# Two AdaLN blocks on one core: the setup ahead of the attention moved into the hand-written order of slots

## The chip, the core and the metric

The kernel runs on one core of a Trainium2 chip. The time is device microseconds of one launch. Five runs of the kernel before gave a median of 1122.37 us (1118.46 to 1125.07). The engines are PE (TensorE), DVE (VectorE), ACT (ScalarE), POOL (GpSimd) and SP (SyncE), which only issues DMAs here.

## What is computed

Two transformer blocks on `x` of 8 batches, 512 tokens and 128 channels, all in 32-bit floats. Only the start of the first block matters for the change:

```python
mod = (_silu(L0_c) @ L0_wmod).reshape(L0_c.shape[0], 6, 1, -1)
sa, ca, ga, sb, cb, gb = (mod[:, i] for i in range(6))
ga = (2 * (ga >= 0) - 1) * jnp.maximum(jnp.abs(ga), 0.25)   # gb likewise
h = _layernorm(x, axis=-1) * (1 + ca) + sa
x = x + ga * attention(h)        # 16 heads of 8 channels, weights W + 2 B A (low rank)
h = _layernorm(x, axis=-1) * (1 + cb) + sb
x = x + gb * mixture_of_experts(h)
```

The second block has the same frame with a state-space layer and another mixture of experts, and its own `mod`.

## The kernel before, in words

**Setup (lines 97 to 350).** Batches lie as tiles `x0` to `x7`, 128 tokens on partitions, four chunks. SP loads the columns `pc` (L103) and all eight batches (L107). ACT issues `wqkvo`, `lora` and `wmod` (L114 to L118), POOL twelve later weights (L120 to L143). DVE makes the constants (`tri`, `ones`, `before`, `count`, `mask`, `spare`), POOL clears `zeros`, four `mpad` tiles of 128x512 (L185) and two `vaug` tiles of 128x2048. PE makes the modulation of both layers (L210, two times six matmuls of 128x128 by 8 columns), the low-rank product (L232), the output bias (L237), and the gate rows (L249): four tensors of a row per batch, each as two groups of four 128x128 matmuls that spread a column over all partitions; ACT copies each group to `ga_rows`, `gab_rows`, `sb_rows`, `cb_rows` (L252). DVE takes the statistics of all eight batches (L261, L262). `finish_stats` then makes all 32 reciprocal roots at once: ACT Sqrt (L265) and DVE reciprocal (L266).

In this part a scheduler chooses the order of the instructions on each engine: its order is not that of the program. The statistics of eight batches stand mixed with the modulation on DVE, and Sqrt behind the first five gate-row copies on ACT.

**Attention (from L350).** From here the order is written out by hand: the wrapper `InOrder` (its line, L65, stands for all instructions issued through it) pins each engine to program order, and PE's matmuls are pinned one by one. Work is told off in slots. `slot(s)` issues two score matmuls `ps` (from slot 0 on, L474) and one pair `pm` (L446), whose row maxima DVE takes (`mpad<-pm`), twelve slots ahead of the scores (`LEAD` is 6 steps of two slots); then the Exp of the scores on ACT (`es<-ps`), and what `at_slot` has put behind this slot. `pm` has two buffers, the one-bank PSUM tiles (`bank`) four. A `pm` or `ps` matmul has 32 rows of the array, and two or four of them stream side by side; transposes, projections and gate rows use all 128 rows.

For batch 0, `load_batch` normalises the four chunks on POOL (`xh`, slot -30), PE transposes them (`ptn`), ACT modulates (`ht`), PE projects (`pqk`, L406), ACT evicts `qf` and `kf`, and `split` masks four heads of a group (`qt`, `kt`) on POOL. The first slot with PE work is -12. `max_done` transposes the maxima of a group (`pmt`, L462, slot -3 for the first) and DVE subtracts them from `qt`. Every 32 slots are a batch. In slots 0, 2, ... SP also issues sixteen fills of 1 MB that zero `x_rows`, which the mixture of experts scatters into from slot 84 on.

## Time and profile before

| | us |
|---|---|
| median of five runs | 1122.37 |
| the profiled execution, its own time | 1121.07 |
| its span, first to last instruction | 1119.3 |
| PE busy | 1023.3 (91%) |
| DVE busy | 665.0 (59%) |
| ACT busy | 633.4 (57%) |
| POOL busy | 471.1 (42%) |
| DMA, mean over the span | 81 GB/s |
| mean granted clock of TensorE | 0.945 |

A busy share is a mean over stages of different kinds; a busy PE is not PE at its peak, since matmuls are pipelined and their ends are modelled. The granted clock is the share of full speed that PE was given. In the timeline a row has its start, its length, engine, line, operation, output and input, the number of instructions merged into it, and in brackets the idle time of that engine ahead of it and what ended it. A matmul in 32-bit floats has two records, a transpose one.

### The profile page before, as it was taken

The numbers are of one execution on the slowest core, as the hardware profiler recorded it, in microseconds if no ns is written. First come the engines' busy times: TensorE is split into PE (matmuls) and PEld (weight loads), VectorE is DVE, ScalarE is ACT, GpSimd is POOL, SyncE is SP. The second block draws the span as 40 slices with busy tenths as digits, with TensorE's granted clock in tenths as the row PEclk, the third lists the DMA queues.
The fourth block names the chain that finished last, engine by engine and source line by source line (L and its number), as shares of the span: only waits on it lengthen the run. The fifth ranks groups of instructions, "written<-read, shape, count | busy, mean of one in ns | idle before, by whom it ended". The sixth has DMA issues, their size and how long they took to land. (4 is left out here: it accounts for less than half of the span.)

```text
span 1119.3 us, 24186 instructions
## 1 busy us (share of the span) xinstructions
PE 1023.3 (91%) x9540; PEld 667.8 (60%) x9540; DVE 665.0 (59%) x1356; ACT 633.4 (57%) x1378; POOL 471.1 (42%) x723
## 2 busy tenths in 40 slices
PE   6799999999999999999989999959989956878887
PEld 6255555555555555555579999747778724444555
DVE  4377776776777777777420023026676469697563
ACT  2156666676766667666735565324576544555543
POOL 4401223462544546352463033436432374456570
PEclk9589999999999999999989999959999977989999
DMA  9960000000000000000047677511553032232241
GB/s 305 283 175 2 2 1 12 1 28 4 16 16 9 23 5 28 1 28 4 16 151 203 179 200 203 145 38 43 146 145 101 8 107 77 76 95 96 81 145 38
DMA packets 92033, 90.60 MB, mean 81 GB/s; under 512 B 6769, under 2 KB 71353, under 8 KB 91921
## 3 DMA queue, kind: packets, MB, share of 16 engines
q1 hardware_dynamic: 86928, 78.31, 23.7%
q0 software_dynamic: 4688, 9.68, 2.8%
q8 instruction: 75, 1.23, 0.5%
q10 hardware_dynamic: 304, 1.08, 0.3%
q14 instruction: 38, 0.30, 0.1%
HBM read 57.71 MB, written 31.33 MB: 80 GB/s over the span
## 5 line engine op out<-in xcount | busy, mean ns | idle before, releaser
L65 DVE TENSOR_REDUCE mpad<-pm 128x2 f32<-128x1024 f32 x256 | 309.8, 1221 | 136.5 <-PE pm L446 122.7
L65 ACT ACTIVATE es<-ps 128x512 f32<-128x512 f32 x512 | 275.1, 598 | 157.1 <-PE pm L446 111.6
L474 PE MATMUL ps<-qt,kt 32*128 32x512 f32 x1024 | 292.5, 635 | 0.1
L446 PE MATMUL pm<-kt,qt 32*128 32x512 f32 x1024 | 280.6, 664 | 4.5 <-POOL kt L65 2.4
L495 PEld LDWEIGHTS av<-es,vaug 128*32 128x32 f32 x4096 | 104.3, 109 | 94.4 <-ACT part L65 41.0
L495 PE MATMUL av<-es,vaug 128*32 128x128 f32 x4096 | 138.2, 276 | 0.0
L474 PEld LDWEIGHTS ps<-qt,kt 32*128 32x128 f32 x1024 | 95.3, 185 | 61.1 <-issue 33.3
L65 ACT ACTIVATE hid<-ph,bias 128x256 f32<-128x256 f32 x184 | 72.2, 477 | 56.7 <-PE ph L947 55.0
L708 POOL DMA_INDIRECT x_rows<-tok,ux x64 | 64.4, 1007 | 75.9 <-DMA x_rows<-tok,ux 69.6
L958 PEld LDWEIGHTS pyb<-w2b,hid 128*128 128x128 f32 x736 | 91.1, 194 | 6.0 <-ACT hid L65 3.3
L958 PE MATMUL pyb<-w2b,hid 128*128 128x128 f32 x736 | 91.8, 278 | 2.9 <-ACT hid L65 2.9
L446 PEld LDWEIGHTS pm<-kt,qt 32*128 32x128 f32 x1024 | 79.6, 190 | 24.6 <-DVE mpad L65 11.2
L947 PE MATMUL ph<-xt,w1b 128*128 128x256 f32 x368 | 89.6, 387 | 1.9 <-issue 1.9
L65 POOL TENSOR_SCALAR qt<-qf,mask,zero 128x512 f32<-128x512 f32 x32 | 24.6, 769 | 149.8 <-PE pm L446 128.4
L978 POOL DMA_INDIRECT yg<-y_rows,yrows x64 | 63.1, 987 | 35.6 <-issue 17.9
L65 DVE COPY xt<-pxt 128x256 f32<-128x256 f32 x46 | 19.4, 421 | 98.3 <-PE pxt L873 80.0
L947 PEld LDWEIGHTS ph<-xt,w1b 128*128 128x128 f32 x368 | 68.0, 195 | 9.8 <-issue 2.1
L1374 PE MATMUL pe<-x,l1w_sb 128*128 128x512 f32 x128 | 71.4, 666 | 0.5 <-ACT ye L65 0.3
L65 ACT ACTIVATE ye<-pe,pc 128x512 f32<-128x512 f32 x64 | 43.4, 683 | 40.5 <-PE pe L1374 31.7
L65 POOL TENSOR_TENSOR t<-t 128x512 f32<-128x512 f32 x34 | 49.3, 1450 | 36.3 <-DVE t L65 21.3
L65 DVE TENSOR_TENSOR t<-ye,gb 128x512 f32<-128x512 f32 x64 | 53.2, 848 | 4.6 <-POOL t L65 4.6
L1362 PE MATMUL r<-l1w_sb,t 128*128 128x128 f32 x240 | 33.9, 287 | 14.7 <-POOL t L65 9.4
(318 smaller groups left out, 1537.2 us busy)
## 6 DMA issues: line engine op xcount, KB each, us to landing
x_rows<-zeros SPq DMA_DIRECT2D x16, 1024.0 KB
gb<-g_rows SPq DMA_DIRECT2D x32, 512.0 KB
w1b<-in_w1t SPq DMA_DIRECT2D x46, 256.0 KB
w2b<-in_w2t SPq DMA_DIRECT2D x46, 256.0 KB
xg<-x_rows SPq DMA_DIRECT2D x46, 128.0 KB
y_rows<-yb SPq DMA_DIRECT2D x46, 128.0 KB
x<-in_x SPq DMA_DIRECT2D x8, 256.0 KB
h_chan<-hf SPq DMA_DIRECT2D x8, 256.0 KB
```

The costliest lines, as they stand in the source:

```text
L65: return lambda *args, **kwargs: self.pin(call(*args, **kwargs))
L446: T.matmul(pm[:, i, :], lhsT=qt[r : r + 32, qc * P : (qc + 1) * P], rhs=kt[r : r + 32, :], start=True, stop=True,)
L474: T.matmul(ps, lhsT=kt[r : r + 32, kc * P : (kc + 1) * P], rhs=qt[r : r + 32, :], start=True, stop=True)
L495: T.matmul(ps[32 * j : 32 * j + 32, 0, :], lhsT=vaugs[b % 2][:, kc, 4 * j + m, :], rhs=es_of[4 * g + kc, j][:, q], start=(kc == 0), stop=( ...
L708: nc.gpsimd.indirect_dma_start(out=x_rows[h], out_offset=IndirectOffsetOnAxis(ap=chosen["ux", b][:, k, c : c + 1], axis=0), in_=half[h]["t ...
L947: pin(T.matmul(ph[:, f, :], lhsT=it["w1"][:, f * P : (f + 1) * P], rhs=it["x"], start=True, stop=True))
L958: T.matmul(py[:, c, :], lhsT=it["hid"][:, f, c * P : (c + 1) * P], rhs=it["w2"][:, f, :], start=(f == 0 and "shared" not in it), stop=(f = ...
L978: nc.gpsimd.indirect_dma_start(out=gathered[b][:, k, c, :], out_offset=None, in_=y_rows[h], in_offset=IndirectOffsetOnAxis(ap=half[h]["yro ...
L1362: T.matmul(ffn[b]["r"][:, c, :], lhsT=x[:, c * P : (c + 1) * P], rhs=w, start=(start and c == 0), stop=stop, skip_group_check=True,)
L1374: pin(T.matmul(pe, lhsT=l1w_sb[:, 2 + e, :], rhs=x1s[b], start=True, stop=True))
```

## The change

- The whole setup is pinned to program order on DVE, ACT, POOL and SP; PE's setup matmuls are pinned too.
- SP loads `pc`, `x0`, then `wmod` of layer 0 in two pieces, `x1`, `wmod` of layer 1, the other batches and after them the twelve later weights, which POOL issued before. ACT issues `wqkvo` and `lora` (two pieces). The early weights no longer have a pool of their own; they use buffers of `es`.
- `zeros`, `mpad` and `vaug` are cleared on DVE instead of POOL.
- Statistics are taken one batch per 32 slots (`load_stats`, slots 32b-40 to 32b-37), and the roots per batch (`load_root`, slot 32b-35) by a power on POOL and a Newton step, on DVE for batch 0 and on POOL for the others. Sqrt, its table and the reciprocal go.
- Silu comes at slot -42, the low-rank product at -34, layer 0's modulation at -33. Its gate clamp (-11), the output bias (-10), layer 1's modulation (-9) and clamp (-8) come behind the first `pm`. The eight gate-row groups are one per slot from -8 to -1.
- Batch 0's `xh` and the first group's `qt` and `kt` are made on DVE instead of POOL; batch 0 gets `gab_rows` at slot -2 instead of -27.

On PE the order is now: low-rank product, modulation 0, `ptn`, `pqk`, three slots of `pm`, bias, a slot of `pm`, modulation 1, and then `pm`, gate-row group, in turn, eight times; `pmt` stands between the `pm` and the gate rows of slot -3.

```diff
-    V, A, G, T, Q = nc.vector, nc.scalar, nc.gpsimd, nc.tensor, nc.sync
+    pin = tc.keep_in_program_order
+    V, A, G, Q = (InOrder(e, pin) for e in (nc.vector, nc.scalar, nc.gpsimd, nc.sync))
+    T = nc.tensor
...
-    G.memset(zeros, 0.0)
+    V.memset(zeros, 0.0)
...
-        G.memset(mp, 0.0)
+        V.memset(mp, 0.0)
...
-    def finish_stats(mv, rstd):
-        A.activation(rstd, mv[:, :, 1], AF.Sqrt, bias=eps5)
-        V.reciprocal(rstd, rstd)
...
-    for b in range(B):
-        stats(xs[b], mv1, b)
-    finish_stats(mv1, rs1)
...
-            G.memset(va, 0.0)
-            G.memset(va[:, :, :, HD], 1.0)
+            V.memset(va, 0.0)
+            V.memset(va[:, :, :, HD], 1.0)
...
+        wmod_sb = []
+        for layer in range(2):
+            parts = []
+            for c0 in range(0, 6 * D, S):
+                w = min(S, 6 * D - c0)
+                t = early([P, w], f"wmod{layer}")
+                Q.dma_start(out=t, in_=wmod[:, layer, c0 : c0 + w])
+                parts += [t[:, k * D : (k + 1) * D] for k in range(w // D)]
+            wmod_sb.append(parts)
+            load_x(layer + 1)
+        for b in range(3, B):
+            load_x(b)
+        load_later()
...
+        def mod_rows(src, dst, b0):
+
+            pg = bank("prow")
+            for b in range(b0, b0 + 4):
+                pin(
+                    T.matmul(
+                        pg[:, b - b0, :], lhsT=src[:, b : b + 1].to_broadcast([P, P]), rhs=ident, start=True, stop=True
+                    )
+                )
+            A.copy(dst[:, b0 : b0 + 4, :], pg)
...
+        def load_root(b):
+            r = rs1[:, b * NC4 : (b + 1) * NC4]
+            on = V if b == 0 else G
+            root_end(r, root_begin(r, mv1[:, b * NC4 : (b + 1) * NC4, 1], 1e-5, on=on), on=on)
...
-                    G.tensor_scalar(
+                    (V if b == 0 else G).tensor_scalar(
...
+            on = V if g == 0 else G
+            on.tensor_scalar(qt, batch[b]["q"], mask[:, m : m + 1], zero, ALU.mult, ALU.add)
+            on.tensor_scalar(kt, batch[b]["k"], mask[:, m : m + 1], spare[:, sp : sp + 1], ALU.mult, ALU.add)
...
+        at_slot(-42, silu_c)
+        at_slot(-34, low_rank)
+        at_slot(-33, lambda: modulation(0, mod0))
+        at_slot(-11, lambda: clamp(mod0, MOE_SCALE))
+        at_slot(-10, out_bias)
+        at_slot(-9, lambda: modulation(1, mod1))
+        at_slot(-8, lambda: clamp(mod1, None))
+        rows = ((gab, gab_rows), (mod0[:, 2, :], ga_rows), (mod0[:, 3, :], sb_rows), (mod0[:, 4, :], cb_rows))
+        for i, (src, dst) in enumerate(rows):
+            for b0 in range(0, B, 4):
+                at_slot(-8 + i + b0, lambda src=src, dst=dst, b0=b0: mod_rows(src, dst, b0))
...
+            for c in range(NC4):
+                at_slot(32 * b - 40 + c, lambda b=b, c=c: load_stats(b, c))
+            at_slot(32 * b - 35, lambda b=b: load_root(b))
+            for i, s in enumerate((-30, -27 if b else -2, -24)):
```

## The prediction, on record before the run

> **What bounds the kernel now.** I read first the 40 slices of the page, to see where engines, clock and transfers change, then the timeline of the first 75 us, where the change lies, and last a table of busy time by stretches cut to the steps of the granted clock.

> ```profile
> PE   6799999999999999999989999959989956878887
> PEclk9589999999999999999989999959999977989999
> DMA  9960000000000000000047677511553032232241
> ```

> The reader is to see that PE is full from slice 3 to half of the span, while the first two slices (28 us each) are setup: PE waits there, and in slice 2 its clock stands at half. What the setup loses is lost to the end, since the attention behind it keeps PE full. The DMA row is near 9 in the same slices, mostly the zero fill of `x_rows` (16 x 1 MB), which nobody needs until the first scatter (slot 84).

> In the timeline I follow the last waits up to the first matmul of the pipeline (`pm`, slot -12):

> ```profile
> 25.68 0.58 ACT L252 COPY sb_rows<-p 128x512 f32<-128x512 f32 x1 [0.31 <-PE p L249]
> 26.29 1.28 ACT L265 ACT_TABLE_LOAD   x1
> 27.58 0.32 ACT L265 ACTIVATE rstd_l0a<-mv_l0a,eps 128x32 f32<-128x32 f32 x1
> ...
> 27.93 0.35 DVE L266 RECIPROCAL rstd_l0a<-rstd_l0a 128x32 f32<-128x32 f32 x1 [4.59 <-ACT rstd_l0a L265]
> ...
> 28.40 3.15 POOL L65 TENSOR_SCALAR xh<-x,mv_l0a,rstd_l0a 128x128 f32<-128x128 f32 x4 [6.54 <-DVE next L65]
> ...
> 32.16 0.78 ACT L65 ACTIVATE ht<-ptn,mod 128x512 f32<-128x512 f32 x1 [2.81 <-issue]
> ...
> 36.81 0.69 ACT L65 ACTIVATE qf<-pqk,bqs 128x512 f32<-128x512 f32 x1 [3.87 <-PE pqk L406]
> 37.40 0.68 ACT L65 ACTIVATE kf<-pqk,pc 128x512 f32<-128x512 f32 x1
> ...
> 38.35 0.79 POOL L65 TENSOR_SCALAR kt<-kf,mask,spare 128x512 f32<-128x512 f32 x1
> ...
> 39.19 2.09 PE L446 MATMUL pm<-kt,qt 32*128 32x512 f32 x8 [2.42 <-POOL kt L65]
> ```

> One batch's roots wait for the statistics of all eight, and the square root waits on ACT behind five gate-row copies and a table load. Only at 28.40 does batch 0 start, and at 39.19 the first `pm`. Slot 0 (first `ps`, after a `qt` update) streams at 59.43: 20.2 us for twelve slots, 1.7 each.

> **The clock in this stage.** The records of the clock begin at 23.94 (the 1.00 that the views show earlier is a default: 16 gate-row records of L249 took 3.76 us at 18.20 and 32 took 3.74 us at 24.59). It changes only at multiples of 3.41 us from there. Columns: PE, PEld, DVE, ACT, POOL busy, then granted clock.

> ```profile
> 34.18:37.59 3.41, 2.60 (x4) 0.50 (x2) 0.00 (x0) 0.78 (x2) 0.00 (x0) 0.50 0.97 283
> 47.83:51.24 3.41, 3.21 (x12) 1.01 (x8) 2.36 (x2) 0.00 (x0) 0.00 (x0) 0.50 0.97 282
> 58.07:61.48 3.41, 3.41 (x14) 1.18 (x8) 2.32 (x3) 0.10 (x1) 0.00 (x0) 0.50 0.98 283
> 61.48:64.90 3.42, 3.42 (x18) 2.07 (x16) 1.80 (x3) 1.59 (x4) 0.00 (x0) 0.50 0.97 280
> 64.90:68.31 3.41, 3.41 (x30) 1.87 (x24) 2.41 (x3) 2.68 (x6) 0.00 (x0) 1.00 0.97 283
> ```

> Busy time does not decide: 3.21 of 3.41 us busy leaves the clock at half. What sorts the steps is how much of the array streams. A record of 512 columns streams 0.853 us at half clock, one of 128 columns 0.213, weighted by its rows over 128. A window of `pm` alone (32 rows) uses 0.50 of the array, 34.18 and 58.07 use 0.70, and all stay at half; 61.48, with `ps` and `pm` side by side, uses 0.99 and is followed by full clock. Over the whole trace every half-clock window up to 0.70 stayed and every one from 0.83 up was released (0.83 at 948.95, a quarter of the array's time in it being transposes, so these count); full-clock windows below 0.31 fell back and from 0.44 up stayed.

> **The setup, new path.** In program order DVE sets the pace. It does the small constants of before (0.81 to 1.2 us), waits for `ident` (2.53 in before, behind one DMA issue that goes: about 1.6), then the scan, mask and counts, as 15.40 to 16.3 and 1.18 to 1.6 of before: to 3.0. New on DVE are POOL's memsets. DVE's own rows give 0.11 us for 64 and 0.17 for 128 elements, about 1 ns an element: four `mpad` of 512, 2.1, and two `vaug` of 2048 with their ones, 4.4: 9.6 with `next`. POOL's rows (0.54 and 1.80) would give 9.0; two elements a step, as DVE's 0.45 us for a 32x512 TENSOR_SCALAR suggests, 6.4. I take 9.6, from the nearest rows. Statistics of batch 0 alone: 4 x 0.26, 10.7. `x0` landed at 5.06 in before, so its transfer is covered by 4 us. The root: DVE 0.2, POOL power 1.05 to 1.44 (`rstd_l0f`, `rr`), four DVE steps of 0.2: 13.0. Then `wqk` 0.6, `bqs`, `mod` copy and two adds 0.3, and `xh` on DVE, four of 0.2 to 0.28: 14.8, against 3.15 us on POOL. The modulation matmuls (12 records of 0.22 us after a weight that should land by 6) are done by 9. From the last `xh` to `ht` before took 0.62 us, from `ht` to `kf`'s end 5.92, all the same; `kt` on DVE 0.46 to 0.8 in place of 0.79 after a `qt`. First `pm` at 21.9 in place of 39.19: **-17.3 us**, between -14.5 (POOL-like small steps) and -20 (fast memsets). Neither table load nor Sqrt is on this path; the Exp table load (1.28) moves behind the last gate-row copy, where `ps` of slot 0 streams beside it.

> **What the slots take over.** PE is in order, so work put into slots -10 to -1 stands between `pm` and `pm`. Eight gate-row groups of 8 records: 1.71 us each at half clock. A change between 32-row and 128-row work also drains:

> ```profile
> 56.02 1.12 PE L462 MATMUL pmt<-ident,mpad 128*128 128x128 f32 x4
> 57.07 2.57 PE L446 MATMUL pm<-kt,qt 32*128 32x512 f32 x8
> ```

> By the records, `pm` stopped streaming at 55.88, `pmt` streamed from 56.08 to 56.93, `pm` from 57.23: gaps of 0.2 and 0.3. A slot with a row group thus takes 1.71 + 0.2 + 1.71 + 0.3 = 3.9 us at half clock against 1.7: 2.2 x 8 = 17.7. The second modulation (12 x 0.213 and a drain, 3.1), the bias matmul (0.8) and the first slots' lost overlap (1.8) make 23.4. DVE's additions there (17 small operations at 0.08, four statistics at 0.27) fit under PE's 3.9 a slot. ACT's eight copies of 0.59 too. Bounds: nothing, if the rows ran in holes (PE has 0.2 us idle in 3.41, so no), to 23.4.

> [...]

> How much of the 23.4 comes back hangs on the clock. A row slot uses (1.71 + 0.85) / 3.9 = 0.65 of the array, a best-placed window 0.71: just above what stayed. At slot -3 the transposes `pmt` (0.85) stand beside a row group (1.71): such a window reaches 0.83 if it lies right, 0.75 in nearly half of the placements. If released there, the last two row slots cost 4.2 in place of 8.0, and the first scores, at half clock for 5.5 us in before, save 2.7: 23.4 - 6.5 = **+16.9**.

> **The rest.** Seven batches' statistics (4 x 0.27 each) go onto DVE inside the attention, and seven roots of some 2.3 us onto POOL, which there waits 87 us for `pm`. DVE is busy 36 of 50 us, PE paces: of at most 7.4 us I take **+1.2**; a gain I exclude, as nothing leaves. The 12 later weights (SP, about 0.4 us an issue) now stand ahead of the zero fill, same bytes, needed 100 us later: 0. `gab` is added to `x0` late (slot -2), on POOL, before splits that have 5 us to spare: 0.

> **Sum.** -17.3 + 16.9 + 1.2 = +0.8 on the profiled execution's 1121.07 us (span 1119.3). The median of before is 1.30 above it, so 1122.37 + 0.8 = **1123.2**.

> **The rivals.**
> *Cold to slot 0 (slower).* No window reaches the bound, because transposes and rows straddle two. Then 23.4 stand, less 0.8 for a release soon after slot 0: -17.3 + 22.6 + 1.2 = +6.5, 1128.9. It decides as soon as the clock is still at half when the first `ps` streams. For it: 0.65 is below 0.70.
> *Early release (faster).* The bound lies near 0.70 and the second row slot ends it: six row slots at 2.0 instead of 3.9 save 11.4, `pmt` 0.4, the first scores 2.7: -17.3 + 8.9 + 1.2 = -7.2, 1115.2. For it: 0.71 is in reach of the bound.
> *Setup does not shorten.* A transfer on the shared queue (x0, or weights for `mod`) lands later than DVE needs it; it must be 5 us late to matter, and each us costs one. At 5 us more: 1128.

> [...]

> **How the numbers follow.** Late release 0.42 (its own range 1119 to 1127, by the setup's bounds); cold 0.33; early release 0.19; setup not shorter 0.06. A difference of 0.3% (3.4 us) is what a measurement can tell here. Faster by that: early release and 0.08 of the late one, 0.27. Slower: 0.31 of cold, 0.07 of late, 0.03 of the last, 0.41. Same: 0.32. The range, from the early release with a larger setup gain to cold with a smaller one: 1113 to 1131.

> **What would show it.** First `pm` at 21 to 23 us; `vaug` memsets of about 2 us on DVE; row slots of 3.9 us while the clock is at half; a release next to `pmt` of slot -3; first `ps` near 61 (65 if cold, 53 if early). I am wrong if the clock is full in the first row slots, if gate rows stream beside `pm`, or if the attention's batches (62.1 us from `es` to `es` of 32 slots now) lengthen by over 1 us each.

## The result, and the profile after

The changed kernel took 1124.5 us (median of 36 runs, 1120.47 to 1130.21) beside 1120.86 us for the kernel before in the same series (62 runs, 1117.19 to 1125.08): a ratio of 1.0032 with a 95% interval of 1.0023 to 1.0041, slower by 0.3% or 3.6 us. The profiled execution took 1125.72 us, its span is 1123.9.

The 40 slices of the changed kernel:

```profile
PE   4999999999999999999979999859989966968887
PEclk9999999999999999999989999969899977889999
DMA  9970000000000000000047677511543032222241
```

In slice 2 PE is full, where it waited before. The clock row is no help there: the records of this execution begin at 59.43, and ahead of them the views show full clock whatever it was. The lengths tell it: eight records of 128 columns take 1.16 us at full clock, 2.08 at half.

The timeline of the same kernel, up to the first `pm` (start, length, engine, line, operation, output and input, idle time ahead):

```profile
5.46 2.00 DVE L65 MEMSET vaug<- 128x2048 f32 x2 [0.38 <-issue]
...
9.77 0.29 DVE L65 BATCH_NORM_STATS2 bnst<-x 128x6 f32<-128x128 f32 x1
10.19 0.26 DVE L65 BATCH_NORM_STATS2 bnst<-x 128x6 f32<-128x128 f32 x1
...
11.74 1.02 POOL L65 TENSOR_TENSOR rstd_l0a<-var,mhalf 128x4 f32<-128x4 f32 x1 [10.32 <-DVE var L65]
...
23.02 1.23 PE L469 MATMUL pm<-kt,qt 32*128 32x512 f32 x4 [2.20 <-DVE kt L65]
```

DVE paces this stretch without a pause over 0.4 us up to the statistics, and POOL idles for 10.3 us until DVE has a variance. `pm` starts at 23.0, 16.2 us ahead of before. The row slots of the same kernel, on PE:

```profile
51.67 2.08 PE L385 MATMUL prow<-ident,gab 128*128 128x128 f32 x8
53.68 2.08 PE L469 MATMUL pm<-kt,qt 32*128 32x512 f32 x4
55.69 1.12 PE L485 MATMUL pmt<-ident,mpad 128*128 128x128 f32 x4
56.59 1.91 PE L385 MATMUL prow<-ident,mod 128*128 128x128 f32 x8
58.44 1.60 PE L469 MATMUL pm<-kt,qt 32*128 32x512 f32 x4
59.97 1.16 PE L385 MATMUL prow<-ident,mod 128*128 128x128 f32 x8
...
63.20 0.70 PE L497 MATMUL ps<-qt,kt 32*128 32x512 f32 x2
```

From 35.62 on `pm` and gate rows alternate every 4.0 us at half clock; the clock is full from 59.43, the end of the window (one of the 3.41 us steps of the clock) that holds most of `pmt`, and the last row slot takes 2.14. The first `ps` streams at 63.20, before at 59.43: the 16.2 us won ahead of the first `pm` are lost, and 3.8 more, in the twelve slots behind it.

Where the rest goes is read from the distance of like instructions in the two traces (ACT's, counted back from the last). It needed more than one profile of each kernel; the others are among the experiments. All distances are to the first profile of before, in us:

| | at 100 us | at 560 | at 600 | at the end |
|---|---|---|---|---|
| before, second profile | +0.1 | 0.0 | +0.5 | +3.0 |
| before, third profile | +1.3 | +1.0 | +1.4 | +4.4 |
| changed kernel | +2.0 | +1.7 | +3.5 | +4.6 |
| changed kernel, again | +0.7 | +0.6 | +2.4 | -0.7 |

Three things are to be seen. From 60 to 100 the changed kernel makes up 1.8 us of what it lacked at the first `ps`, since its clock is full by then and that of before isn't until 64.9. Between 100 and 560 nothing is lost to the statistics in the attention. Between 560 and 600, where the attention ends, the changed kernel loses 1.8 us, in both of its profiles; before loses at most 0.4. What comes behind 600 spreads by 4 us between executions of one kernel and says nothing on the change.

### The profile page after: what moved, and what is told of

It reads as the page before. It is cut to its first block, busy times and chain, and to the rows that moved or that the text cites. A ratio compares the mean times of both kernels' runs of the same rounds, so it can differ in the third digit from the quotient of the medians.

```text
span 1123.9 us, 24218 instructions
## 1 busy us (share of the span) xinstructions
PE 1030.0 (92%) x9540; PEld 671.2 (60%) x9540; DVE 677.7 (60%) x1373; ACT 632.5 (56%) x1376; POOL 470.3 (42%) x739
## 5 line engine op out<-in xcount | busy, mean ns | idle before, releaser
L65 DVE TENSOR_REDUCE mpad<-pm 128x2 f32<-128x1024 f32 x256 | 310.6, 1219 | 128.6 <-PE pm L469 128.1
L65 ACT ACTIVATE es<-ps 128x512 f32<-128x512 f32 x512 | 275.0, 598 | 134.9 <-PE pm L469 112.8
L65 ACT ACTIVATE hid<-ph,bias 128x256 f32<-128x256 f32 x184 | 72.2, 477 | 58.0 <-PE ph L985 55.6
L65 DVE COPY xt<-pxt 128x256 f32<-128x256 f32 x46 | 19.3, 421 | 98.1 <-PE pxt L911 84.8
L65 POOL TENSOR_SCALAR qt<-qf,mask,zero 128x512 f32<-128x512 f32 x31 | 24.1, 776 | 125.9 <-PE pm L469 100.3
L985 PEld LDWEIGHTS ph<-xt,w1b 128*128 128x128 f32 x368 | 67.9, 195 | 10.3 <-issue 2.2
L65 ACT ACTIVATE ye<-pe,pc 128x512 f32<-128x512 f32 x64 | 43.4, 683 | 40.7 <-PE pe L1412 31.9
L65 POOL TENSOR_TENSOR t<-t 128x512 f32<-128x512 f32 x34 | 49.5, 1457 | 36.3 <-DVE t L65 21.3
L65 DVE TENSOR_TENSOR t<-ye,gb 128x512 f32<-128x512 f32 x64 | 53.2, 848 | 4.6 <-POOL t L65 4.6
L996 PE MATMUL pyb<-ws,hid 128*128 128x128 f32 x256 | 39.1, 299 | 15.2 <-issue 14.9
```

Source lines behind the costliest of these rows:

```text
L65: return lambda *args, **kwargs: self.pin(call(*args, **kwargs))
L985: pin(T.matmul(ph[:, f, :], lhsT=it["w1"][:, f * P : (f + 1) * P], rhs=it["x"], start=True, stop=True))
L996: T.matmul(py[:, c, :], lhsT=it["hid"][:, f, c * P : (c + 1) * P], rhs=it["w2"][:, f, :], start=(f == 0 and "shared" not in it), stop=(f = ...
```

## Experiments

The theory: two costs meet. DVE's chain sets the first `pm`; behind it the gate rows are serial with `pm` on PE, and a row slot costs 4.0 us rather than 2.1 because a mix of `pm` and rows uses too little of the array to bring the clock back (0.65 to 0.67 in the four windows of the changed kernel from 35.53 to 49.19, an estimate made as in the prediction). The main rival: the clock is no part of it, rows cost what they cost. The runs fell on four chips (before takes 1092 to 1093 us on two of them, 1121 to 1124 on the others), so times are compared as ratios to before on the same chip; a distance to the changed kernel is that ratio over 1.0032.

| kernel | first `pm` | first `ps` | ratio to before, 95% interval |
|---|---|---|---|
| changed kernel again | 22.9 | 61.9 | 1.0030, 1.0010 to 1.0049 |
| rows in one block, early | 30.1 | 50.3 | 0.9925, 0.9901 to 0.9948 |
| clears on POOL | 18.6 | 57.7 | 1.0019, 0.9997 to 1.0040 |
| no rows | 23.0 | 48.3 | 0.9911, 0.9887 to 0.9934 |
| fillers | 21.1 | 61.5 | 0.9941, 0.9908 to 0.9974 |
| more fillers | 21.1 | 49.4 | 0.9900, 0.9883 to 0.9917 |
| rows early, clears on POOL | 27.4 | 47.4 | 0.9894, 0.9880 to 0.9909 |
| the same, with fillers | 26.7 | 49.6 | 0.9893, 0.9879 to 0.9908 |
| the same, clamp late | 26.9 | 44.9 | 0.9867, 0.9842 to 0.9892 |
| later weights on POOL | 23.0 | 66.5 | 1.0029, 1.0011 to 1.0048 |

**Rows in one block ahead of the first `pm`.**

```diff
-                at_slot(-8 + i + b0, lambda src=src, dst=dst, b0=b0: mod_rows(src, dst, b0))
+                at_slot(-15, lambda src=src, dst=dst, b0=b0: mod_rows(src, dst, b0))
```

(The first clamp and the bias move ahead with it, to slot -23, and the second modulation to -14.)

> All eight groups of gate-row matmuls are put in one block after the first projections and ahead of the first power product pm, instead of one group beside each of eight slots. Theory (the eight row groups are serial on PE and slow only because the clock is at half while pm and rows alternate at 0.50 to 0.67 of the array): the rows run dense, 8 x 1.7 = 13.7 us at half clock or less, the first pm moves from 23.0 to 29 to 31, the twelve slots ahead of the first ps then cost 1.2 to 1.7 us each without rows, and the first ps starts at 46 to 51 instead of 63.2; the time is 8 to 15 us under the changed kernel's. Rival (the rows cost the same wherever they stand, and the clock is no part of it): first ps within 2 us of 63.2, time within 0.3% of the changed kernel's.

The gate rows on PE, in this kernel's timeline:

```profile
20.62 2.97 PE L385 MATMUL prow<-ident,gab 128*128 128x128 f32 x16
23.43 5.52 PE L385 MATMUL prow<-ident,mod 128*128 128x128 f32 x48
```

The 64 records take 8.3 us in all: they follow the projections without a gap, and the clock is full from 22.74, where the first dense window ends. `pm` starts 7.1 us later, `ps` 12.9 us earlier, the time is 1.1% or 12 us under the changed kernel's, as expected. The rival is out: where the rows stand decides their price. (The clamp, the bias and the second modulation moved with them and have a part in the figure.)

**No rows.** The gate-row matmuls and copies are left out, and the rows are filled with 0.5, so the gates are not computed.

```diff
-                at_slot(-8 + i + b0, lambda src=src, dst=dst, b0=b0: mod_rows(src, dst, b0))
+                at_slot(-8 + i + b0, lambda dst=dst, b0=b0: G.memset(dst[:, b0 : b0 + 4, :], 0.5))
```

> The gate-row matmuls and their copies are left out, and the rows are filled with 0.5 by GpSimd: the gates are not computed. Theory (the row groups cost what stands on PE ahead of the first ps): first ps at 45 to 48 instead of 63.2, some 15 us less, and the time 13 to 17 us under the changed kernel's, with the attention's batches as long as before. Rival (the start is set by the statistics and by the chain from pm to es, with the rows in its shadow): first ps not more than 5 us earlier.

The first `ps` at 48.34 is 14.9 us ahead of the changed kernel, the time 13.6 us under it. Against it the dense block costs 2.0 us at the first `ps` (the bias and the second modulation, which moved along, take less there and lower the figure); spread over the slots the same rows cost 14.9.

**Fillers.** Two kernels put matmuls of no use on PE ahead of the rows.

```diff
+        def fill_pe(n):
+            for _ in range(n):
+                pin(T.matmul(flat(bank("fill")), lhsT=ident, rhs=xs[0].rearrange("p c d -> p (c d)"), start=True, stop=True))
...
+        at_slot(-32, lambda: fill_pe(3))
+        at_slot(-15, lambda: fill_pe(2))
+        for s in (-12, -11, -10):
+            at_slot(s, lambda: fill_pe(1))
```

> Filler matmuls of no use (128x512, into a spare bank) are put on PE: three after the first modulation, two after the first projections, one in each of the three slots ahead of the rows, so that the array is busy over 0.75 of a window before the rows start. Theory (the half clock is what makes a row slot 4.0 us): the clock is full by the first row slot, a row slot takes 2.1 to 2.4 us, first ps 8 to 13 us ahead of 63.2, less the fillers' own 2 to 3 us, and the time 6 to 12 us under the changed kernel's. Rival (a row slot is long for its number of instructions, or for its copies, not for the clock): row slots stay at 3.5 us or more and the time rises by the fillers, 2 to 4 us.

The twelve times fall into two groups: five from 1079.1 to 1082.0, seven from 1091.4 to 1096.6. The profiled execution is of the upper one. Its windows (PE, PEld, DVE, ACT, POOL busy, granted clock) show why:

```profile
28.20:31.61 3.41, 3.41 (x24) 2.25 (x21) 2.25 (x6) 0.00 (x0) 0.00 (x0) 1.00 0.93 279
31.61:35.02 3.41, 3.41 (x12) 1.68 (x10) 2.43 (x12) 0.59 (x1) 0.00 (x0) 0.50 0.98 290
```

The clock had been full before the first row slot and fell there: PE counts as busy for all of 3.41 us, but the records in it, the twelve eight-column ones of the second modulation among them, use 0.30 of the array by the same estimate. To see whether this window parts the two groups, the second kernel puts one more filler on each side of that modulation:

```diff
+        at_slot(-9, lambda: fill_pe(1))
         at_slot(-9, lambda: modulation(1, mod1))
+        at_slot(-9, lambda: fill_pe(1))
```

> As the kernel with fillers in the changed order, with two more fillers around the second modulation, whose window had used 0.30 of the array and let the clock fall in the profiled run. Theory (its times of 1079 to 1082 and of 1091 to 1097 are runs that kept the full clock through the row slots and runs that lost it there): now every run keeps it, row slots take 2.1 to 2.4 us, first ps at 50 to 53, and the times lie in one group within 3 us of the lower one, some 14 to 17 us under the changed kernel's. Rival (the two groups come from somewhere else, behind the attention): two groups again, about 12 us apart.

One group: five times from 1106.5 to 1112.2 on a chip where before takes 1120.89, 0.990 of it, where the lower group had stood at 0.989 (its median 1081.49 over 1093.25). The spread of 5.7 us is wider than the 3 expected, with no gap in it. The row slots take 2.0 to 2.2 us, 2.6 with `pmt`:

```profile
32.91 1.16 PE L385 MATMUL prow<-ident,gab 128*128 128x128 f32 x8
34.00 1.13 PE L473 MATMUL pm<-kt,qt 32*128 32x512 f32 x4
```

The order and the work of the changed kernel, with ten useless matmuls added, take 1.3% or 15 us less. The half clock is shown to be the cause, and the rival of the first filler kernel, that a row slot is long for its instructions or copies, is out. That the upper group of the first filler kernel is the one that loses the clock rests on one profiled execution of it, on the level of the second kernel, and on the granted clocks on record: 0.966 to 0.970 in the five executions of the lower group, 0.951 to 0.961 in the seven of the upper, where 34.1 us at half clock in the profile are worth 0.016 of the mean. No execution of the lower group was profiled.

**The clears.**

```diff
-    V.memset(zeros, 0.0)
+    G.memset(zeros, 0.0)
...
-        V.memset(mp, 0.0)
+        G.memset(mp, 0.0)
...
-            V.memset(va, 0.0)
-            V.memset(va[:, :, :, HD], 1.0)
+            G.memset(va, 0.0)
+            G.memset(va[:, :, :, HD], 1.0)
```

> The clearing of zeros, mpad and vaug goes back to GpSimd, which idles up to 10.3 us in the changed kernel; all else stays. Theory (the chain on DVE sets the first pm, and the three clears of 2.1, 2.0 and 1.8 us stand in it): the statistics start some 6 us earlier, the power step then waits for GpSimd or the modulation's copy, first pm at 17 to 19 instead of 23.0, first ps at 57 to 60, time 4 to 6 us under the changed kernel's. Rival (GpSimd's clears take as long there and hold up its power step, or the loads of x bound the statistics): first pm stays within 1 us of 23.0, no difference in time.

The first `pm` comes at 18.63, 4.4 us earlier, and the first `ps` at 57.69: the clears stood in DVE's chain, as the theory has it. The time did not follow, where 4 to 6 us were expected: the profiled execution, 1089.83, is the shortest of twelve that reach to 1099.15, and the median lies 1.5 us under the changed kernel's by the ratios. None of the others was profiled, but their granted clocks on record fall into two groups: six executions, the profiled one among them, at 0.946 to 0.955 (median time 1092.4), six at 0.965 to 0.974 (1097.1). The mean is higher where an execution's clock records begin later, since full clock is counted ahead of them: in the profiles of the changed kernel it is 0.944 with records from 20.39, 0.958 with records from 59.43. So in half of the executions the windows lay differently; that these lost the clock at their row slots fits their times and is not shown.

**Both edits, and the clock held.** The two edits together, then with the second modulation between the fourth and the fifth row group and a filler of 256 columns at every second `pm`, then with the second clamp moved to slot 40 and fillers in each of the slots -8 to -5.

> Both edits that moved the first ps forward, together: the eight gate-row groups in one block behind the first projections, and the clears on GpSimd. Theory (they are independent: one takes 13 us from the slots, the other 4.4 from the chain ahead of the first pm, which is partly the rows' cover now): first pm at 24.5 to 27, first ps at 44 to 47, time 13 to 18 us under the changed kernel's. Rival (only the rows count for the end, since the clears alone took 5.5 us from the first ps and little from the median time): time as with the rows alone, about 11.7 us under the changed kernel's.

27.4 and 47.4, each 0.4 us past the range expected, and a time 15.5 us under the changed kernel's by the ratios. It has the lowest ratio of the kernels without useless work, and is faster than before by 1.1%.

```diff
         at_slot(-8, lambda: clamp(mod1, None))
+        for s in range(-12, 0, 2):
+            at_slot(s, lambda: fill_pe(1, 256))
```

> As the kernel with both edits, and the clock held: the second modulation stands between the fourth and the fifth row group, and a filler matmul of no use (128x256) beside every second pm of the twelve slots ahead of the first ps, so that no window falls below 0.44 of the array. Theory (dense rows bring the clock to full, and pm alone, at 0.35 to 0.5, lets it fall): the clock stays full from the rows to the first ps, those slots take 1.2 to 1.4 us, first ps at 39 to 43, time 18 to 24 us under the changed kernel's. Rival (these slots are bound by DVE's maxima, whatever the clock): first ps within 1.5 us of the kernel without fillers.

A miss: first `ps` at 49.6, time as without fillers. The timeline on PE:

```profile
37.02 1.13 PE L473 MATMUL pm<-kt,qt 32*128 32x512 f32 x4 [0.88 <-DVE mpad L65]
...
40.35 1.22 PE L393 MATMUL fill<-x,ident 128*128 128x256 f32 x2
```

The clock held until PE had to wait for DVE's maxima (0.88 us here), in the slots where DVE also takes batch 1's statistics and layer 1's clamp. The window at 35.6 used 0.25 of the array by estimate and the clock fell; the filler at 40.35 takes 1.22 us, at full clock 0.70.

```diff
-        at_slot(-8, lambda: clamp(mod1, None))
-        for s in range(-12, 0, 2):
+        at_slot(40, lambda: clamp(mod1, None))
+        for s in (-12, -10, -8, -7, -6, -5, -4, -2):
```

> As the kernel with dense rows, clears on GpSimd and fillers, with layer 1's gate clamp moved from slot -8 to slot 40 and a filler (128x256, of no use) in each of the slots -8 to -5, where DVE took 1.6 us a slot and the window fell to 0.25 of the array. Theory (the clock fell there because PE stood waiting for DVE, and the last five slots ahead of the first ps ran at half clock for it): the clock now stays full to the first ps, which starts at 43 to 46 instead of 49.6, and the time falls by 4 to 6 us, to some 0.985 of the kernel before. Rival (DVE sets these slots at any clock, and the fillers only add to them): first ps at 48 or later, time as without this edit.

The first group's transposes on PE:

```profile
41.65 0.66 PE L489 MATMUL pmt<-ident,mpad 128*128 128x128 f32 x4
```

(In the changed kernel 1.12.) The clock is full from 19.0 to 551.5, and the first `ps` comes at 44.9. The time is 0.9867 of before, the lowest ratio of all and 3 us under the kernel with the clamp early, where 4 to 6 were expected; the two intervals meet, so that the order of the last three kernels in time isn't settled. In the trace 17.1 us are won at 560 and only 13.1 are left at 600. That is the stretch in which the changed kernel had lost 1.8.

**The end of the attention.** To see whether that loss is chance, the changed kernel was run once more, and before was profiled twice more.

> The changed kernel once more, nothing edited. Theory: first pm at 23.0, the first four or more row slots at 4.0 us, first ps at 61 to 65 (66 or 67 where no window beside pmt is released), time 2 to 5 us over the kernel before; what the first 63 us do not explain of a run's time comes from the granted clock behind the attention, so that two runs of this kernel differ there by steps of 1.5 to 3 us. Rival (the change also lengthens the stages behind the attention): the two traces of the changed kernel stand alike there, and both behind the kernel before by 2.9 us.

> The kernel before once more, nothing edited, for its profile. Question: 2 us of the distance between the two kernels arises between 565 and 600 us, where the profiled run of before had two windows of half clock and the changed kernel's had three. Theory (chance of how the windows lie): a new profile of before may have three, and is then 1.5 to 3 us later there against its own first ps; behind 720 us it differs from the first profile by steps of up to 5 us. Rival (the change itself delays the first transfers behind the attention): before again has two windows and stands within 0.5 us of its first profile at 600.

> The same once more: a third profile of the kernel before. Theory and rival as for the other look; with three profiles of before beside the changed kernel's two, two windows in all three would speak for the rival.

The two traces of the changed kernel are 1.1 us apart at 600 and 5.3 at the end, so what lies behind 600 is chance to that extent, as the theory had it. Between 560 and 600 the rival won: two windows of half clock in all three profiles of before, three in both of the changed kernel. SP's queue has the difference first. Of before, then of the changed kernel, the first gather of rows for the experts and the issue of the second expert's weights:

```profile
564.99 0.41 SPq L65 DMA_DIRECT2D xg<-x_rows  x1
...
568.86 0.33 SPq L65 DMA_DIRECT2D w1b<-in_w1t  x1
```

```profile
566.74 0.41 SPq L65 DMA_DIRECT2D xg<-x_rows  x1
...
571.11 0.34 SPq L65 DMA_DIRECT2D w1b<-in_w1t  x1
```

The weights are issued 3.87 us behind the first gather in before (3.98 and 3.95 in its other profiles), 4.37 in the changed kernel, and 4.22 to 4.47 in all ten profiles that have the change (4.47 in the one taken on the chip of the other two of before). Counted as in the table, these ten lose 0.8 to 4.0 us from 560 to 600 (1.3 to 3.7 from 565; the expectation of the last run has 1.3 to 4.4). On PE the transposes of the third gather and, behind the first dense stretch, `py`, first in before, then in the changed kernel:

```profile
573.48 0.66 PE L873 MATMUL pxt<-ident,xg 128*128 128x128 f32 x2 [0.89 <-DMA xg<-x_rows]
...
577.13 1.05 PE L538 MATMUL py<-wo,ot 128*128 128x128 f32 x8
```

```profile
575.83 0.66 PE L911 MATMUL pxt<-ident,xg 128*128 128x128 f32 x2 [1.62 <-DMA xg<-x_rows]
...
579.70 1.92 PE L561 MATMUL py<-wo,ot 128*128 128x128 f32 x8
```

The transposes wait 1.62 us for their gather instead of 0.89, the dense stretch `ph` begins that much later and gets its clock one window later, and `py` still runs at half clock (1.92 against 1.05). The last run undoes the part of the change that touches SP ahead of this:

```diff
-        load_later()
+        for i, load in enumerate(later):
+            at_slot(4 + 2 * i, load)
```

(`later` holds the twelve loads of `load_later`, issued by POOL.)

> One part of the change undone: the twelve later weights are issued by GpSimd again, one in every second slot from slot 4, instead of by SyncE ahead of the zero fill; all else is the changed kernel. Question: in each of the ten profiles of kernels with the change, SyncE issues the second expert's weights 4.2 to 4.5 us behind the first gather of rows after the attention, in three of before 3.9 to 4.0, and 1.3 to 4.4 us are lost between 565 and 600. Theory (the twelve issues shift what SyncE has in front of it there): now 3.9 to 4.0 us, two windows of half clock, not over 0.6 us lost there, first ps at 61 to 65 as in the changed kernel, and the time 1.5 to 3 us under the changed kernel's. Rival (another part of the change, or its place in the program, does it): 4.2 to 4.5 us, three windows, and a time within 0.2% of the changed kernel's.

SP's queue in this kernel:

```profile
570.42 0.41 SPq L65 DMA_DIRECT2D xg<-x_rows  x1
...
574.08 0.33 SPq L65 DMA_DIRECT2D w1b<-in_w1t  x1
```

3.66 us, and two windows of half clock (575.8 to 582.6); nothing (0.0 us) is lost from 560 to 600 instead of 1.8. So the later issue of the weights goes with the twelve issues on SP, 500 us behind the place where they were put, and they cost up to 1.8 us; the size rests on this one profile, on a chip that no other run shared. The place of the windows has a part in it: the kernel with the rows in one block issues the weights 4.45 us behind the gather and yet has two windows of half clock (562.0 to 568.9) and loses 0.8. How the issues do it stays open: in the changed kernel SP stands 0.5 us between the register move and the issue of these weights, and its records name nothing that it waits for.

The time of this run shows no gain (1.0029), where 1.5 to 3 us were expected, and its profile has the reason for that execution at least. Its PE, beside the row slots of the changed kernel shown above:

```profile
55.69 1.11 PE L484 MATMUL pmt<-ident,mpad 128*128 128x128 f32 x4
56.60 1.91 PE L384 MATMUL prow<-ident,mod 128*128 128x128 f32 x8
...
60.45 2.08 PE L384 MATMUL prow<-ident,mod 128*128 128x128 f32 x8
```

The row slots stand where they stood in the changed kernel, `pmt` at 55.69 in both. But the windows lie at 53.54 and 56.95 here, at 56.01 there. There one window holds `pmt` and most of a row group, by estimate 0.80 of the array; here they are split, 0.61 and 0.65, the clock stays at half until 70.6, and the first `ps` comes at 66.47. Two executions with one order on PE, the same starts within 0.01 us up to 58.44, and 3.3 us apart at the first `ps` by where the window fell.

## Why the prediction was right in the small sum, and where it was wrong

It forecast 1123.2 on a median of 1122.37, +0.8; measured are +3.6, by the interval +2.6 to +4.6, inside the range and on the edge between its cases of no change and slower.

- **First `pm` at 21.9**: right in mechanism, 1.1 us short. The term that failed most in size is "Statistics of batch 0 alone: 4 x 0.26", with 0.7 us of it: in program order a pair takes 0.40 from start to start (9.77, 10.19, ... 11.49), 0.26 was the pace of before, where the pairs overlapped. The clears came out right, 9.77 against 9.6.
- **Row slots of 3.9 us at half clock**: right (4.0). The two gaps at the change of rows are in it, 0.3 us each: in the changed kernel a row group stopped streaming at 37.49, `pm` streamed from 37.79 to 39.49, the next group from 39.79.
- **Late release, first `ps` near 61**: right in two of three profiles of this order (63.2 and 61.9), with the release in the window of `pmt`; the third is the rival *cold* (66.5 for 65). The prediction gave these two cases chances as if the kernel decided between them. It doesn't; the window edge nearest to the start of `pmt` lay 0.32 us behind it in the changed kernel's profile, 0.14 ahead of it in its second and 1.26 behind it in the third. At 100 us the two profiles with the release stand at +2.0 and +0.7, where the forecast, without the statistics, had -0.4.
- **Attention +1.2**: wrong. From 100 to 560 the two profiles change by -0.3 and -0.1. DVE and POOL took the statistics and the roots beside PE; of the bounds, nothing and 7.4 us, the lower one was right, by the row that was named beside it: PE paces.
- **"The 12 later weights ... needed 100 us later: 0"**: this step failed. Its cost doesn't lie in the bytes or in the first 70 us, where the prediction looked, but at the end of the attention: 1.8 us are lost there, and none in the one profile without the twelve issues on SP.
- **Early release** was rightly given little: the first five row slots stayed at half clock in every profile of this order without fillers.

The profiles where the clock is released lack 0.7 to 2.0 us at 100 and 1.8 more behind the attention, 2.4 to 3.5 at 600; the one where it isn't lacks 5.9 at 100, some 4 to 5 more. Together they have the size of the measured 3.6, or somewhat over. That the sum came within 2.8 us of it is in part luck: the start was put too early, the statistics too dear, and the loss behind the attention was not seen. How often the release is missed was not counted, but the granted clocks on record again make two groups: 21 executions of the changed kernel at 0.937 to 0.947, with a median time of 1123.6, and 17 at 0.954 to 0.962, with 1126.1. The two profiles with the release are one of each group, so the groups are not simply released and missed; the 2.5 us between their medians go with where the clock records begin, and so with where the windows lie.

The last experiment shows what the place of the windows is worth: 3.3 us for 0.94 us of displacement. Busy time does not part the windows: in the changed kernel PE was busy without a gap from 35.6 to 59.4, seven windows, at half clock. By the prediction's way of counting, an estimate, the first six used 0.57 to 0.67 of the array, the last 0.80, and full clock followed the last alone.

## What to carry to other kernels

Price work moved on PE by the window it will stand in, not by its records: the same 64 records delayed the first scores by 2.0 us in one dense block (which took the bias and the second modulation along) and by 14.9 beside thin matmuls. In the block the clock came to full at 22.74; the mix ran at half from 35.6 to 59.4; with the clock held by fillers the mix too had its first scores at 49.4, 1.1 us behind the kernel without rows. Where a release hangs on one window (0.80 of the array with it here, 0.61 and 0.65 without), give every case its weight and expect times in groups; with fillers enough for every window the second group was gone (five executions). And when issues move to another queue, follow that queue to the next place where somebody waits for it, however far behind.

## What the runs showed of the hardware

```profile
743.12 0.37 PE L996 MATMUL pyb<-ws,hid 128*128 128x128 f32 x1 [1.73 <-issue]
```

  Why only on these chips isn't known, nor whether these stops make up the whole distance.
